# Score products of the last query block as halves of the TensorE array

## The chip, the cores and the metric

The kernel runs on one core of a Trainium2 chip. A core has five engines that work side by side and meet through semaphores: TensorE (PE, matmuls, with its weight loads shown apart as PEld), VectorE (DVE), ScalarE (ACT), GpSimd (POOL) and SyncE (SP). Each takes its instructions in order. SP computes nothing; here it issues nearly all transfers between memories. The metric is the device time of one execution in microseconds (us). The median of three runs of the kernel before is 1521.35 us (1520.33 to 1521.79).

## The reference

One layer: multi-head latent attention with 16 heads over 2048 tokens of width 512, a residual and a layer norm, then one linear map with a residual and a layer norm. The part that matters here:

```python
cq = rms_norm(hidden_states @ w_qa.T, q_a_ln_w)
q = (cq @ w_qb.T).reshape(b, s, H, DQ).transpose(0, 2, 1, 3)
q_nope, q_pe = (q[..., :DN], q[..., DN:])          # 128 and 64 wide
q_pe = q_pe * cos + rotate_half(q_pe) * sin
ckv = hidden_states @ w_kva.T
k_pe = ... the same rotation of ckv[..., KVLR:], one for all heads
scores = jnp.einsum('bhqd,bhkd->bhqk', q_full, k_full) * scale
scores = jnp.where(causal, -jnp.inf, scores)
attn = jax.nn.softmax(scores.astype(jnp.float32), axis=-1)
out = jnp.einsum('bhqk,bhkd->bhqd', attn, v)
```

## The kernel before

**Number format.** Everything that enters a matmul is a float32 value split into a high and a low float16 part; a product is the sum of high by high, high by low and low by high. The key's up-projection is folded into the query, so all heads share one key table `Kn` (128 rows, high and low) and one rotary table `Kp` (64 rows, written twice: rows 0 to 63 and 64 to 127 hold the same values, high in plane 0 and low in plane 1). A head's rotary query `pe` has its high part in rows 0 to 63 and its low part in rows 64 to 127.

**Blocks.** Queries are worked on in four blocks `b` of 512 (`units`, from L981). Block `b` sees `512 (b + 1)` keys. Within a block the loop runs over 8 pairs `p` of heads, then over four query tiles `qt` of 128, then over the two heads `j` of the pair. One pass of the inner loop is called a head below: 64 of them in block 3, 8 in a pair. In block 3 a head has 1664, 1792, 1920 or 2048 keys for `qt` 0 to 3.

**One head** (`head_scores`, L712). `chunks` cuts the keys into two tiles of two chunks: 512 and 512 columns, then twice 320, 384, 448 or 512. A tile is two PSUM banks. In block 3 three such tiles take turns (`"ssu"[state["turn"]]`), so the second tile of a head is the first tile of the head before it. For each chunk `score` (L680) issues five matmuls of 128 rows: `Kn` high and low with the high query, `Kn` high with the low query, `Kp` high and low with the rotary query. The causal mask is a sixth small matmul for `j = 0` (L695) and an addition on DVE for `j = 1` (L699). DVE then takes each tile's row maximum (L738), a small step makes the bias (L748), ACT takes the exponentials (L754) and sums, DVE the reciprocal (L766, L767).

**The head before it** (`head_probs`, L770) is finished in between: ACT writes the high half of the probabilities (L775, two halves of the row), DVE the low half (L778, two halves), and SP issues one DMA transpose of both into a ring (L782), from which TensorE later takes the products with the values (`values`, L820, matmuls in L831). After the transpose `put_in` issues stores that were put off.

**The order of the work.** In block 3, from `(b, p, qt) = (3, 0, 1)` on, the instructions of TensorE, SP, DVE and ACT stand in the order in which the Python code issues them. For head n this is: its scores on TensorE; on DVE the first maximum, with `qt > 1` the first low half of head n - 1, the second maximum, the bias, the remaining low halves of n - 1; the transpose of n - 1 on SP; the exponentials of n on ACT. Then come `run_soon` (rotary low parts on ACT and POOL), `fill` (a piece of the projections of the next pair: `project_pe` L607, `project_nope` L657) and one half of a `values` product. A projection's rotary rows are gathered by POOL into `pe`.

Of the kernel before, what the change touches and what calls it, by code (L numbers as in the profile page):

```python
# [9 lines left out]
F16 = mybir.dt.float16  # L10
BF16 = mybir.dt.bfloat16
F32 = mybir.dt.float32
F32R = mybir.dt.float32r
AF = mybir.ActivationFunctionType
ALU = mybir.AluOpType
# [4 lines left out]
P = 128  # L20
# [6 lines left out]
QB = 512  # L27
NPAIR = H // 2
# [8 lines left out]
W_O = 32768.0  # L37
X_UP = 1024.0
PROBS = 10240
TINY = 1.0e-30  # L40
NEG = -1.0e30

# [16 lines left out]
def mla_block(ctx: ExitStack, tc: tile.TileContext, a, out):  # L59
    nc = tc.nc  # L60
# [33 lines left out]
    identb = const.tile([P, P], BF16, name="identb")  # L94
    nc.vector.tensor_copy(identb, ident)
    maskb = const.tile([P, P], BF16, name="maskb")
# [28 lines left out]
    Kn = kv.tile([P, 2, S], F16, name="Kn")  # L125
    Kp = kv.tile([P, 2, S], F16, name="Kp")
# [14 lines left out]
    psum = {}  # L141
# [366 lines left out]
    state = {"queue": nc.sync}  # L508
# [85 lines left out]
    def run_soon():  # L594
        while soon:
            soon.pop(0)()
# [104 lines left out]

    def take(n):

        at = state.get("probs_at", 0)
        if at + n > PROBS:
            at = 0
        state["probs_at"] = at + n
        return probs_mem[:, at : at + n]  # L710

    def head_scores(pools, b, p, j, qt, nk, prev):  # L712
        r = er[1][:, p // 2 : p // 2 + 1]
        cks = chunks(nk)
        nt = len(cks)
        neg = small.tile([P, 2], F32, tag="neg", name="neg")
        tiles = []
        for ti, ck in enumerate(cks):

            if b == 2 and ti == 1:  # L720
                ps = psum["t"].tile([P, 1, 512], F32, tag="t", name=f"s{b}_{p}_{qt}_{j}_{ti}", bufs=2)
            else:
                k = "s"
                if b == 3:

                    state["turn"] = (state.get("turn", -1) + 1) % 3
                    k = "ssu"[state["turn"]]
                ps = psum[k].tile(
                    [P, 2, 512], F32, tag=k, name=f"s{b}_{p}_{qt}_{j}_{ti}", bufs=3 if b == 1 else 1 if k == "u" else 2
                )  # L730
            w = ck[0][1]
            for ci, (c0, w) in enumerate(ck):
                d = nk - P - c0
                score(ps[:, ci, :], c0, w, b, p, j, qt, d if 0 <= d < w else None)
            v = ps[:, : len(ck), :w]
            if ti == nt - 1 == 0:
                next(prev, None)
            nc.vector.tensor_reduce(neg[:, ti : ti + 1], v, axis=AX.XY, op=ALU.max, negate=True)  # L738
            tiles.append((v, ck[0][0], len(ck), w))
            if ti < nt - 1:  # L740
                next(prev, None)
                if b < NB - 1 or qt > 1 and (p, qt, j) != (NPAIR - 1, 3, 1):
                    next(prev, None)
        bias = small.tile([P, 1], F32, tag="bias", name="bias")
        if nt == 1:
            nc.vector.tensor_scalar(bias, neg[:, 0:1], r, None, ALU.mult)
        else:
            nc.vector.tensor_scalar(bias, neg[:, 0:1], neg[:, 1:2], r, ALU.min, ALU.mult)  # L748
        for _ in prev:
            pass  # L750
        pr = take(nk)
        sums = small.tile([P, 2], F32, tag="sums", name="sums")
        for ti, (v, c0, n, w) in enumerate(tiles):
            nc.scalar.activation(  # L754
                pr[:, c0 : c0 + n * w].rearrange("p (a c) -> p a c", a=n),
                v,
                AF.Exp,
                bias=bias,
                scale=r,
                accum_out=sums[:, ti : ti + 1],  # L760
            )
        inv = small.tile([P, 1], F32, tag="inv", name="inv")
        if nt == 1:
            nc.vector.tensor_scalar(inv, sums[:, 0:1], 1.0 / P_UP, None, ALU.mult)
        else:
            nc.vector.tensor_scalar(inv, sums[:, 0:1], sums[:, 1:2], 1.0 / P_UP, ALU.add, ALU.mult)  # L766
        nc.vector.reciprocal(inv, inv)  # L767
        return pr, inv
# [114 lines left out]
    with tc.manual_schedule(engines={ET.PE}):  # L883
# [38 lines left out]
        pe = state["pe", 0, 0] = blk.tile([P, 4, QB], F16, tag="pe", name="pe0_0")  # L922
# [58 lines left out]
    def units(pool, ring, b, norms=None):  # L981
        lag = min(ring.shape[1] // (2048 * (b + 1)) - 1, 3) if b else 4

        for p in range(NPAIR):
            put_in(True)


            if p + 1 == NPAIR:
                at = (1, 2, 4, 5) if b < NB - 1 else (1, 3, 5, 7)
            elif p % 2 == 0 and p + 2 < NPAIR:  # L990
                at = (0, 1, 2, 3) if (b, p) == (1, 0) else (0, 1, 3, 4)
            else:
                at = (3, 4)
            if b and p % 2 == 0 and p + 2 < NPAIR:
                fillers.append(project_pe(b, p // 2 + 1))
            if p + 1 < NPAIR:
                fillers.append(project(b, p + 1) if b == 0 else project_nope(b, p + 1))
            elif b + 1 < NB:
                fillers.append(project(b + 1, 0))
            if b == NB - 1 and p == NPAIR - 1:  # L1000
                ctx_p.close()
                pcr = state["pcr"] = ctx.enter_context(
                    tc.tile_pool(name="pcr", bufs=2, side="right", reuse_waits="tile")
                )
                state["wvo"] = [pcr.tile([P, 2, 2, HID], F16, name=f"wvo{p}", bufs=1) for p in range(EARLY)]
                for i in range(EARLY):
                    fillers.append(value_output(i, psum["m"], "m"))
                at = (2, 3, 5, 6)
            for qt in range(4):
                nk = (4 * b + qt + 1) * P  # L1010
                if (b, p, qt) == (NB - 1, 0, 1):
                    ctx_f.enter_context(tc.manual_schedule(engines={ET.PE, ET.SP, ET.DVE, ET.Activation}))
                if (b, p) == (0, NPAIR - 1) and qt >= 2:
                    spare = state["qn", 0, p][:, 2:] if qt == 2 else state["pe", 0, 3][:, 4:]
                    s0 = -4 * nk
                    PT = spare.rearrange("p a b c -> p (a b c)" if qt == 2 else "p a b -> p (a b)")[:, : 4 * nk]
                elif b == 0:
                    s0, PT = -4 * nk, pool.tile([P, 4 * nk], F16, tag=f"PT{qt}", name=f"PT{p}_{qt}")
                else:
                    s0 = room(2048 * (b + 1), ring.shape[1], 4 * nk, (b, p) == (2, NPAIR - 1) and qt > 0)  # L1020
                    PT = ring[:, s0 : s0 + 4 * nk]
                vg = values(b, p, qt, nk, PT)
                if nk <= 512:
                    pi = pair_scores(pool, b, p, qt, nk)
                    probs.append(pair_probs(pool, b, p, qt, nk, PT, *pi))
                    flush()
                    for step in plan[p][qt]:
                        if step == "F":
                            fill()
                        else:  # L1030
                            next(side[step == "W"], None)
                    move_rows(6)
                    run_values(lag)
                    run_values(lag)
                else:
                    for j in range(2):
                        prepare_output(b, p, 2 * qt + j)
                        prev = probs.pop() if probs else iter(())
                        pi = head_scores(pool, b, p, j, qt, nk, prev)
                        probs.append(head_probs(pool, b, p, j, qt, nk, PT, *pi))  # L1040
                        if (b, p, qt, j) == (1, 0, 1, 0):
                            half_values()
                            half_values()
                        run_soon()
                        if 2 * qt + j in at:
                            fill()
                        if b == 2 and (2 * qt + j) % 4 == 2:
                            next(norms, None)
                        run_values(lag)
                vals.append([vg, 0, s0, s0 + 4 * nk])  # L1050
                if b == 0 and qt == 3 and p + 2 < NPAIR:
                    if p % 2 == 0:
                        load_wpe(0, p // 2 + 1)
                    load_wq(0, p + 2)
            drain()
        if b:
            flush()
# [92 lines left out]
    while len(vals) > 2:  # L1150
# [5 lines left out]
    ring = ctx_m.enter_context(tc.tile_pool(name="rings", bufs=1, reuse_waits="tile")).tile(  # L1156
        [P, 12 * 2048], F16, name="ring"
    )
    probs_mem = ctx_m.enter_context(tc.tile_pool(name="probs", bufs=1, reuse_waits="tile")).tile(
        [P, PROBS], F32, name="probs"  # L1160
    )
# [239 lines left out]
```

## Time and profile before

| what | value |
|---|---|
| median of three runs | 1521.35 us |
| the profiled execution, its own time | 1521.0 us |
| its span, first to last instruction | 1519.2 us |
| granted TensorE clock, mean | 0.990 |
| block 3, first score matmul to the end of the last one | 817.1 to 1269.8 us |
| TensorE busy in block 3 | 446.60 of 452.70 us |
| instructions in the trace | 24663 |

The profile is of one execution. Its page gives the busy time of each engine, the chain of work that ended last, followed back from the last instruction, and the costliest groups of instructions by source line. Other views give one engine's instructions in order of time (start, duration, engine, line, operation, what is written and read, and in brackets the idle time before and what ended it), or the busy time of every engine in a stretch, with the granted clock (PEclk) and the share of the DMA engines. A matmul's duration contains its way through the array; the distance between two starts says how fast the array takes them. DMA instructions appear on SP's queue (SPq) with the time for which they occupy it; a transfer lands later.

### The profile page before, as it was taken

The numbers are of one execution on the slowest core, as the hardware profiler recorded it, in microseconds if no ns is written. First come the engines' busy times: TensorE is split into PE (matmuls) and PEld (weight loads), VectorE is DVE, ScalarE is ACT, GpSimd is POOL, SyncE is SP. The second block draws the span as 40 slices with busy tenths as digits, with TensorE's granted clock in tenths as the row PEclk, the third lists the DMA queues.
The fourth block names the chain that finished last, engine by engine and source line by source line (L and its number), as shares of the span: only waits on it lengthen the run. The fifth ranks groups of instructions, "written<-read, shape, count | busy, mean of one in ns | idle before, by whom it ended". The sixth has DMA issues, their size and how long they took to land.

```text
span 1519.2 us, 24663 instructions
## 1 busy us (share of the span) xinstructions
PE 1463.0 (96%) x9116; PEld 915.3 (60%) x9116; DVE 1168.2 (77%) x2181; ACT 938.5 (62%) x1695; POOL 347.3 (23%) x404
## 2 busy tenths in 40 slices
PE   8889988999999999999999999999999989999997
PEld 6667754666665566666666666666666655444445
DVE  5797788888887888888887877877878766465664
ACT  6687775666676777777775675676667665322310
POOL 4223211452216305050033401401300000032132
PEclk9899999999999999999999999999999999999999
DMA  5568774879797898989897788787788798634410
GB/s 202 152 168 202 177 184 108 161 154 173 154 195 152 154 198 177 186 183 180 150 203 146 149 154 164 149 154 153 144 152 183 137 212 186 225 125 127 136 49 35
DMA packets 626536, 242.96 MB, mean 160 GB/s; under 512 B 583024, under 2 KB 603760, under 8 KB 625776
## 3 DMA queue, kind: packets, MB, share of 16 engines
q1 hardware_dynamic: 624960, 239.52, 72.8%
q8 instruction: 71, 1.16, 0.3%
q10 hardware_dynamic: 1152, 1.31, 0.3%
q0 software_dynamic: 304, 0.56, 0.1%
q14 instruction: 49, 0.40, 0.1%
HBM read 67.57 MB, written 28.05 MB: 63 GB/s over the span
## 4 chain that ended last, share of the span: by engine, by line
PE 61%; DVE 3%; DMA 2%; ACT 1%; issue 1%; SPq 0%; POOL 0%; POOLq 0%; ACTq 0%; DVEq 0%
PE s L693 26%; PE o L831 17%; PE acc L1134 10%; PE ps_qn L651 4%; PE ff L1279 3%; PE ps_pe L564 2%; DVE probs L778 1%; DVE neg L738 1%; PE ps_wo L297 1%; ACT probs L754 1%; DMA ring<-probs 1%; DMA fraw<-in_fw_dram 1%; PE tp L1270 0%; DMA wo<-in_wo_dram 0%; ACT probs L775 0%
## 5 line engine op out<-in xcount | busy, mean ns | idle before, releaser
L693 PE MATMUL s<-Kn,qn 128*128 128x512 f16 (+5 forms) x1920 | 462.9, 347 | 10.2 <-DVE qn L73 4.4
L754 ACT ACTIVATE probs<-s,bias,er 128x1024 f32<-128x1024 f32 (+3 forms) x320 | 324.4, 1017 | 209.4 <-DVE bias L748 73.0
L778 DVE SCALAR_TENSOR_TENSOR probs<-probs,inv 128x1024 f16<-128x1024 f32 (+7 forms) x320 | 355.3, 1131 | 26.1 <-ACT probs L775 23.2
L831 PEld LDWEIGHTS <-V 128*128 128x128 f16 x3264 | 319.8, 98 | 86.3 <-issue 12.9
L831 PE MATMUL o<-ring,V 128*128 128x256 f16 x3024 | 362.6, 273 | 2.3 <-DMA ring<-probs 2.0
L738 DVE TENSOR_REDUCE neg<-s 128x1 f32<-128x1024 f32 (+3 forms) x320 | 317.2, 993 | 46.3 <-PE s L693 42.8
L693 PE MATMUL s<-Kp,pe 128*128 128x512 f16 (+5 forms) x1280 | 340.1, 347 | 0.0
L775 ACT ACTIVATE probs<-probs,inv 128x1024 f16<-128x1024 f32 (+7 forms) x320 | 294.2, 959 | 71.1 <-DVE inv L767 52.3
L693 PEld LDWEIGHTS <-qn 128*128 128x128 f16 x1920 | 187.5, 98 | 154.7 <-issue 13.9
L693 PEld LDWEIGHTS <-pe 128*128 128x128 f16 x1280 | 124.8, 98 | 105.8
L651 PE MATMUL ps_qn<-cq,wq 128*128 128x512 f16 (+1 forms) x594 | 138.9, 382 | 5.7 <-DVE qn L73 2.9
L638 POOL TENSOR_TENSOR pe<-prod,ph 32x512 f16<-32x512 f32 x88 | 123.8, 1406 | 5.7
L1134 PE MATMUL acc<-wvo,oh 128*128 128x512 f16 (+1 forms) x424 | 124.1, 375 | 0.9 <-ACT probs L754 0.9
L629 POOL TENSOR_TENSOR prod<-prod 128x512 f32<-128x512 f32 x11 | 14.0, 1269 | 457.4 <-DVE prod L569 457.4
L651 PEld LDWEIGHTS <-wq 128*128 128x128 f16 x594 | 59.3, 100 | 68.1 <-issue 9.3
L1134 PE MATMUL acc<-wvo,ol 128*128 128x512 f16 (+1 forms) x212 | 79.5, 375 | 0.0
L766 DVE TENSOR_SCALAR inv<-sums 128x1 f32<-128x1 f32 x128 | 26.9, 210 | 65.8 <-ACT probs L754 65.2
L564 PE MATMUL ps_pe<-cq,wpe 128*128 128x512 f16 (+1 forms) x306 | 69.5, 373 | 7.4 <-ACT ot L836 4.4
L836 ACT ACTIVATE ot<-o 128x256 f32<-128x256 f32 x128 | 48.4, 379 | 40.7 <-PE o L831 30.1
L72 ACT ACTIVATE xt<-tp 128x512 f16<-128x512 f32 (+1 forms) x17 | 9.7, 572 | 100.3 <-PE tp L1270 86.4
L1134 PEld LDWEIGHTS <-oh 128*128 128x128 f16 x424 | 41.5, 98 | 49.0 <-issue 5.2
L633 POOL CAST pe<-prod 32x512 f16<-32x512 f32 x88 | 66.4, 755 | 12.1 <-PE o L831 8.7
(210 smaller groups left out, 1583.0 us busy)
## 6 DMA issues: line engine op xcount, KB each, us to landing
ot_d<-ot SPq DMA_DIRECT2D x128, 128.0 KB, 2.6
o<-ot_d SPq DMA_DIRECT2D x32, 512.0 KB, 3.7
wq<-wq_d SPq DMA_DIRECT2D x30, 384.0 KB, 3.7
wpe<-wpe_d SPq DMA_DIRECT2D x15, 384.0 KB, 3.9
nw<-in_wo_dram SPq DMA_DIRECT2D x8, 512.0 KB, 4.2
wo<-in_wo_dram SPq DMA_DIRECT2D x4, 1024.0 KB, 6.2
x<-in_x_dram SPq DMA_DIRECT2D x16, 256.0 KB, 3.5
out_dram<-xb SPq DMA_DIRECT2D x15, 256.0 KB, 2.0
```

The lines of the kernel that those rows point to most:

```text
L564: nc.tensor.matmul(ps, w[:, i, lt, x * P : (x + 1) * P], cq[:, tiles(cols), k, lt], start=n == 0, stop=n == 3 * LT - 1)
L633: nc.gpsimd.tensor_copy(pe[32 * x : 32 * x + 32, j, :], rp[q, x, :])
L638: nc.gpsimd.tensor_tensor(pe[64 + 32 * x : 96 + 32 * x, j, :], rp[q, x, :], ph[q, 0, x, :], ALU.subtract)
L651: nc.tensor.matmul(ps, w[:, i, lt, j * P : (j + 1) * P], cq[:, tiles(cols), k, lt], start=n == 0, stop=n == 3 * LT - 1)
L693: nc.tensor.matmul(ps[:, :w], lhs, K[:, i, c0 : c0 + w], start=n == 0, stop=n == 4)
L738: nc.vector.tensor_reduce(neg[:, ti : ti + 1], v, axis=AX.XY, op=ALU.max, negate=True)
L754: nc.scalar.activation(pr[:, c0 : c0 + n * w].rearrange("p (a c) -> p a c", a=n), v, AF.Exp, bias=bias, scale=r, accum_out=sums[:, ti : ti ...
L775: nc.scalar.activation(hl[:, 0, c], pr[:, c], AF.Copy, scale=inv)
L778: nc.vector.scalar_tensor_tensor(hl[:, 1, c], pr[:, c], inv, hl[:, 0, c], ALU.mult, ALU.subtract)
L831: nc.tensor.matmul(ps[:, :256], vt[:, k % 4, i, :], v[:, :, l, k, :], start=n == 0, stop=n == 3 * kts - 1)
L836: nc.scalar.activation(ot, ps[:, :256], AF.Copy)
L1134: nc.tensor.matmul(acc[:, cols], l[:, t, c], state["wvo"][p][:, i, j, cols], start=p == 0 and j == 0 and n == 0, stop=p == NPAIR - 1 and j ...
```

## The change

In block 3 (`b >= ROWS`, with `ROWS = 3`) `head_scores` takes both tiles of a head first and hands all four chunks to a new function. It issues half matmuls of 64 rows: two chunks at a time, one on the lower half of the array's rows, one on the upper half. Each chunk needs nine: both halves of the three `Kn` terms and of the `Kp` high term, and one of the `Kp` low term (the rotary high part only). A chunk's halves must reach its PSUM bank from both sides of the array, so there are two passes: chunks (0, 1), then (2, 3), each with five halves a chunk; then (1, 0) and (3, 2), with four. Between a chunk's two passes an instruction without work on SP reads the bank in name: it waits for the first pass, and the second pass waits for it. In the compiled program these are semaphore instructions on SP; both of head n + 1 stand behind the DMA transpose of head n - 1.

For the upper rows the rotary high part is also needed in rows 64 to 127. `rope_again` copies it there by a DMA on SP once a pair (64 rows of 1024 elements), issued in the second head of the pair before. The mask's matmul comes after all score products, its addition on DVE before the first maximum instead of before the second. The rest of the order of DVE and ACT, and all of POOL, is as before. TensorE has 1024 more matmuls and as many more weight loads.

```diff
+ROWS = 3
+    def rope_again(b, p):
+        again = state["again", b, p] = psum["again"].tile([P, 2, QB], F16, tag="again", name=f"again{b}_{p}")
+        nc.sync.dma_start(again[64:], state["pe", b, p // 2][:64, 2 * (p % 2) : 2 * (p % 2) + 2])
+
+    def scores_by_rows(parts, b, p, j, qt, masked):
+        qs = slice(qt * P, (qt + 1) * P)
+        qn = state["qn", b, p]
+        high, low = qn[:, 0, j, qs], qn[:, 1, j, qs]
+        rope, again = state["pe", b, p // 2][:, 2 * (p % 2) + j, qs], state["again", b, p][:, j, qs]
+        upper = [slice(0, 64), slice(64, P)]
+        left = {n: 9 for n in range(4)}
+        left[3] += masked is not None
+        last = set()
+
+        def add(n, lhs, rhs):
+            ps, c0, w = parts[n]
+            begin = n not in last
+            left[n] -= 1
+            return nc.tensor.matmul(ps[:, :w], lhs, rhs, start=begin, stop=left[n] == 0)
+
+        for lanes in ((0, 1), (2, 3), (1, 0), (3, 2)):
+            first = lanes[0] < lanes[1]
+            ops = [(high, Kn, 0), (high, Kn, 1), (low, Kn, 0), (rope, Kp, 0)]
+            if first:
+                ops.append((None, Kp, 1))
+            for at, (lhs, K, i) in enumerate(ops):
+                for lane, n in enumerate(lanes):
+                    c0, w = parts[n][1:]
+                    rows = upper[lane]
+                    w_ = lhs if lhs is not None else (rope, again)[lane]
+                    ins = add(n, w_[rows], K[rows, i, c0 : c0 + w])
+                    last.add(n)
+            if first:
+                nc.sync.keepalive_nop([nc.sync.lower_ap(parts[n][0][:, : parts[n][2]]) for n in lanes])
+        if masked is not None:
+            ps = parts[3][0]
+            nc.tensor.matmul(ps[:, masked : masked + P], identb, maskb, start=False, stop=True)
...
+        if b >= ROWS:
+            made, parts = [], []
+            for ti, ck in enumerate(cks):
+                state["turn"] = (state.get("turn", -1) + 1) % 3
+                k = "ssu"[state["turn"]]
+                ps = psum[k].tile([P, 2, 512], F32, tag=k, name=f"s{b}_{p}_{qt}_{j}_{ti}", bufs=1 if k == "u" else 2)
+                made.append(ps)
+                parts += [(ps[:, ci], c0, w) for ci, (c0, w) in enumerate(ck)]
+            d = nk - P - parts[3][1]
+            scores_by_rows(parts, b, p, j, qt, d if j == 0 else None)
+            if j:
+                dg = parts[3][0][:, d : d + P]
+                nc.vector.tensor_tensor(dg, dg, maskb, ALU.add)
         for ti, ck in enumerate(cks):
-            if b == 2 and ti == 1:
+            if b >= ROWS:
+                ps = made[ti]
+            elif b == 2 and ti == 1:
...
+                        if b >= ROWS and (qt, j) == (0, 1) and p + 1 < NPAIR:
+                            rope_again(b, p + 1)
+                        if b == ROWS - 1 and p == NPAIR - 1 and (qt, j) == (3, 0):
+                            rope_again(ROWS, 0)
...
+    psum["again"] = ctx_m.enter_context(tc.tile_pool(name="again", bufs=2, reuse_waits="tile"))
```

More of the change, by code (lines that the diff above doesn't have):

```diff
@@ L39 @@
 PROBS = 10240
+ROWS = 3
+SYNC = mybir.DependencyInfo(mybir.DependencyClass.Sync, mybir.DependencyReason.DATA)
 TINY = 1.0e-30
@@ L732, in head_scores @@
             for ci, (c0, w) in enumerate(ck):
+                if b >= ROWS:
+                    continue
                 d = nk - P - c0
```

## The prediction

> **What bounds the kernel now.** I read the page's header and chain first, then block 3 alone by windows, then SP's queue and one DVE stretch in order of time, and last the windows around the few places where TensorE stood still.
>
> ```profile
> PE 1463.0 (96%) x9116; PEld 915.3 (60%) x9116; DVE 1168.2 (77%) x2181; ACT 938.5 (62%) x1695; POOL 347.3 (23%) x404
> PE 61%; DVE 3%; DMA 2%; ACT 1%; issue 1%; SPq 0%; POOL 0%; POOLq 0%; ACTq 0%; DVEq 0%
> ```
>
> TensorE is busy nearly throughout, and the chain that ends last is its own work. SP has no share in it. In block 3 (first row; then pairs 1 and 2 alone) this is sharper:
>
> ```profile
> 817.10:1269.80 452.70, 446.60 (x2867) 280.46 (x2865) 354.06 (x508) 298.82 (x439) 60.86 (x54) 0.99 0.80 158
> 873.40:928.00 54.60, 54.60 (x359) 34.68 (x357) 42.55 (x63) 36.98 (x54) 0.00 (x0) 1.00 0.84 157
> 928.00:986.50 58.50, 58.50 (x377) 36.45 (x375) 47.15 (x67) 37.92 (x55) 20.27 (x18) 1.00 0.79 153
> ```
>
> The stretch is its first figure, TensorE's busy time the second: a pair of heads takes 56.55 us on the mean of an odd and an even one, all of it TensorE. So any time saved on TensorE counts, and any new wait of TensorE counts too. The change brings such a wait, on SP, so SP's queue matters:
>
> ```profile
> L782 SPq DMA_TRANSPOSE ring<-probs x64: 3614/4492/7202, 819.3 to 1267.2; - x64
> ```
> ```profile
> 951.91 3.90 SPq L782 DMA_TRANSPOSE ring<-probs  x1
> 955.86 0.57 SPq L522 DMA_DIRECT2D ot_d<-ot  x1
> ...
> 1149.95 4.49 SPq L782 DMA_TRANSPOSE ring<-probs  x1
> 1154.49 0.57 SPq L522 DMA_DIRECT2D ot_d<-ot  x1
> 1157.40 4.68 SPq L782 DMA_TRANSPOSE ring<-probs  x1
> 1162.18 0.60 SPq L522 DMA_DIRECT2D ot_d<-ot  x1
> ```
>
> The line before this second fence gives the least, median and greatest time of block 3's 64 transposes; the rows are start, duration, instruction. A transpose holds SP 4.49 us, and what is next starts 0.05 us after its end: SP is in order and busy while a transpose is issued. Today no compute engine waits on SP itself, only on transfers that have landed.
>
> **The change, part by part.** *Fewer slots.* A head's scores are 20 matmuls, five per key chunk. Rows of 512 columns start 216 ns apart (five from 879.41 to 880.49 us), of 320 columns 136 ns; for 384 and 448 columns I take 163 and 189. Afterwards they are 36 half matmuls in 18 pairs. Per pair of heads the scores take 2 x 5 x (4 x 2 x 0.216 + 2 x (0.136 + 0.163 + 0.189 + 0.216)) = 31.4 us; a tenth is 3.1 us, over 8 pairs 25 us, if a pair takes one slot. No row shows two halves at once. The ends are 216 ns (wholly together) and 432 ns (one after the other); I take 216, the only slot the rows have, and keep 432 for the range. The 16 additional weight loads a head (98 ns each) run beside matmuls, as 60% of the span already does; a 128-column matmul with its load takes some 55 ns (the mask's, 989.72 to 989.77 us), so two loads and two matmuls fit in a slot of 136 ns. Switching between whole and half array is bounded by nothing and by one matmul's drain, 379 - 216 = 163 ns, twice a head; it falls into the idle time found below.
>
> [...]
>
> *The new wait.* The first pass puts chunk 0 on the lower and chunk 1 on the upper rows (5 pairs), then chunks 2 and 3 (5 pairs); the second pass swaps lanes (4 + 4). Before each swap TensorE waits for an SP no-operation, which waits for the first pass. In SP's order both no-operations of head n+1 stand behind the transpose of head n-1, because that transpose is put in after the scores of head n. It waits for the second low-part split (L778) of n-1 on DVE, which stands behind both maxima (L738) of head n, and the maximum of the first tile needs its second pass. So a ring closes: second pass of n, maxima of n, splits of n-1, transpose of n-1 on SP, no-operation of n+1, second pass of n+1. Before, no step of TensorE hung on SP.
>
> DVE's steps in their present order:
>
> ```profile
> 1153.09 1.28 DVE L778 SCALAR_TENSOR_TENSOR probs<-probs,inv 128x1024 f16<-128x1024 f32 x1 [0.16 <-ACT probs L775]
> 1154.29 0.29 DVE L699 TENSOR_TENSOR s<-s,maskb 128x128 f32<-128x128 f32 x1
> 1154.62 1.22 DVE L738 TENSOR_REDUCE neg<-s 128x1 f32<-128x1024 f32 x1
> 1155.88 0.27 DVE L748 TENSOR_SCALAR bias<-neg,er 128x1 f32<-128x1 f32 x1
> 1156.07 1.27 DVE L778 SCALAR_TENSOR_TENSOR probs<-probs,inv 128x1024 f16<-128x1024 f32 x1
> ```
>
> *The ring's time for a pair of heads (8 heads).* Second pass on tile one, 8 x 4 x 0.216 = 6.9. For the four heads with j = 1 the mask is now added before the first maximum, so both tiles must be finished: 4 x (0.216 + 0.189 + 0.163 + 0.136) = 2.8, and the addition 4 x 0.33 = 1.3. From TensorE's last slot to DVE, 0.16 of drain and 0.04 of handover: 1.6. Maxima 8 x 1.22 + 2 x (0.82 + 0.96 + 1.09 + 1.22) = 18.0. Bias 8 x 0.27 = 2.2. Two splits a head, by the group rows of these two pairs (1146, 1359, 1211, 1278 ns for 832, 896, 960, 1024 elements), 4 each: 20.0. Transposes 8 x 4.49 = 35.9. Behind them four stores of 0.62, a wq load of 0.43, half a wpe load and the new copy of the rotary high rows (one per pair, 128 KB, taken like a store): 3.8. Handovers, some 0.35 a head by the gaps of 0.03 to 0.05 between these rows: 2.8. The sum is 95.3 us against 56.55: 38.75 more, over 8 pairs 310 us.
>
> Nothing covers this: TensorE's own work is 56.55 - 3.1 = 53.4 us a pair, so it would idle 42 us, some 5 us a head. The 25 us saved on it lie in that idle time, and so do values and projections. DVE, ACT and DMA do the same work with more room. The copies' data is ready (POOL fills a rotary group in the even pair before, and is at 0.00 in pair 1, where the first such copy stands), and the first one, in block 2, delays SP by about 0.6 us that nobody waits for.
>
> *The clock.* Idle TensorE loses its clock (third figure from the right: PEclk):
>
> ```profile
> 242.10:245.50 3.40, 0.00 (x0) 0.00 (x0) 3.05 (x8) 0.08 (x1) 0.00 (x0) 1.00 0.84 193
> 245.60:248.90 3.30, 3.04 (x8) 1.12 (x8) 0.67 (x3) 2.81 (x7) 0.00 (x0) 0.50 0.12 40
> ```
>
> After a gap of 4.40 us the next 3.4 us ran at half clock, eight matmuls in 3.40 us. Pauses of 5 us a head would repeat that. In the ring only the second passes can slow down: between 0 and 6.9 + 2.8 = 9.7 us a pair, 0 to 78 us in all. I take half, 39 us, since the half-clock stretch need not meet the second pass.
>
> [...]
>
> The profiled execution took 1521.0 us (span 1519.2), the median of the runs is 1521.35. 1521.0 + 310 + 39 = 1870.
>
> **The rivals.** *A, halves do not overlap.* 432 ns a pair: second passes grow by 9.7 us a pair, 78 us, to 103.6 a pair, still above TensorE's own 53.4 + 28.3; 1948, more with half clock. Nothing in this trace speaks for or against it.
>
> *B, transposes hold SP for less once they come alone.* For: their times vary (3614 to 7202). Against: 951.91 came 4.9 us after the one before and still took 3.90, no less than its size mostly takes. At three quarters 72 us less, about 1800; at half, about 1725.
>
> *C, the SP wait costs nothing, and PSUM alone binds.* A head's second tile is the first tile of the head before, free after its exponential. It is now wanted 5 slots after the scores begin (1.08 us), not 10, and the maxima come later. For a j = 1 head of 2048 keys: 13 pairs 2.8, drain 0.26, mask 0.33, maximum, split, maximum 3.7, bias 0.39, exponential with its handover 1.35 make 8.8 us against 6.6 now; with j = 0, 7.6 against 6.7. With the like for shorter rows and the larger of ring and TensorE for each head, about 60.3 us a pair: +30 us, 1551. It needs SP free when the no-operation is due, which the 4.49 us speak against.
>
> *D, faster.* All new waits lie beside other work and the 25 us come: 1496. The place is the no-operation: it decides for this if SP reaches it within the 5 pairs of the second group, 1.08 us, and C's ring is also covered.
>
> **How the numbers follow.** My forecast 0.58, its own range 1800 to 1930; A 0.18; B 0.13; C 0.07; D 0.03; no visible change 0.01. A tenth more or less on the transposes moves the sum by 29 us. Below 1760 lie C, D, no change and a little of B (0.13), above 1960 part of A (0.06). A measurement of this kernel tells 0.2%, 3 us, from no change: faster 0.03, same 0.01, slower 0.96.
>
> **What would show it.** Right: in block 3 a pair of heads near 95 to 100 us; TensorE busy about 60% there and idle in front of swapped passes, released by SP; no-operations on SP starting right after a transpose ends; PEclk clearly under 0.99 in block 3; transposes still near 4.5 us; blocks 0 to 2 unchanged to within 3 us. Halves overlapping show as pairs starting a few ns apart and slots of 216 ns. Wrong: pairs of heads near 60 us (C) or 53 us (D), or slots of 432 ns (A), or transposes clearly under 4 us (B).

## The result, and the profile after

The changed kernel takes 1836.93 us (median of four runs, 1832.17 to 1839.1); the kernel before took 1521.36 us beside it. The ratio is 1.207, with a 95% interval of 1.205 to 1.210: 316 us slower. The profiled execution took 1839.1 us, its span is 1837.3 us and its mean granted clock 0.923 (before 0.990).

The head of the page of the changed kernel: busy time and instructions of each engine, and the chain that ended last by engine.

```profile
PE 1558.5 (85%) x10140; PEld 929.8 (51%) x10140; DVE 1160.4 (63%) x2181; ACT 937.8 (51%) x1695; POOL 335.2 (18%) x404
PE 31%; SPq 11%; DVE 5%; issue 4%; ACT 3%; POOL 0%; POOLq 0%; ACTq 0%; DVEq 0%
```

SP's queue, which had 0% of the chain, now has 11%. TensorE's share of the span fell from 96% to 85%, and yet its busy time rose by 95 us. The reason shows in block 3 by windows (stretch, its length, busy time of PE, PEld, DVE, ACT and POOL, then PEclk, the share of the DMA engines, GB/s). The first row is the whole block, the second goes from the first exponential of pair 1 to that of pair 3, so two pairs of heads:

```profile
814.80:1586.60 771.80, 541.53 (x3902) 294.48 (x3901) 347.92 (x512) 302.13 (x444) 49.49 (x54) 0.83 0.48 96
924.20:1116.70 192.50, 138.98 (x988) 75.34 (x986) 87.34 (x129) 74.87 (x109) 16.49 (x18) 0.84 0.47 93
```

In the kernel before, block 3 begins 2.7 us earlier than the 817.1 us named ahead of the prediction: its first head, the first with chunks of 320 columns, starts at 814.42. That kernel's TensorE in order of time, and the whole block by windows:

```profile
814.42 0.81 PE L693 MATMUL s<-Kn,qn 128*128 128x512 f16 x3
816.58 0.57 PE L693 MATMUL s<-Kn,qn 128*128 128x320 f16 x3
```
```profile
814.40:1269.80 455.40, 449.30 (x2881) 281.85 (x2880) 354.66 (x512) 301.00 (x443) 60.86 (x54) 0.99 0.80 158
```

So block 3 took 455.40 us and now takes 771.80, 316 more; what lies ahead of it is as long as before to 0.4 us, and what lies behind is 1.3 us longer. Two pairs took 113.1 us (54.60 + 58.50) and now take 192.5. DVE and ACT are busy for about as long as before: they do the same work and wait longer. The granted clock is 0.83, so some 260 us of the block, (1 - 0.83) x 2 x 771.8, ran at half clock (PEclk 0.50), where the pairs of half matmuls of 512 columns in the second passes start 0.43 us apart, the second 0.38 us behind the first, instead of 0.215.

The waits of the changed kernel between 820 and 1580 us (who waited for whom: sum in us, times, longest):

```profile
PE s L726 <- SPq L741: 204.5, 61, 8.5
DVE s L772 <- PE s L726: 186.8, 30, 8.7
DVE neg L797 <- PE s L726: 162.4, 33, 6.8
PE s L726 <- ACT probs L813: 19.8, 16, 1.9
```

L726 is the half matmuls, L741 the no-operations, L772 the mask's addition, L797 the maxima. 61 of the 64 heads wait on SP in this stretch, 3.4 us each, and DVE waits for the scores once a head: by the mask's addition (about half of the heads) or by the first maximum. Now one head in order of time, SP's queue first, then TensorE, then DVE (start, duration, instruction, and in brackets the idle time before and what ended it):

```profile
1204.47 4.80 SPq L841 DMA_TRANSPOSE ring<-probs  x1
1209.36 0.54 SPq L524 DMA_DIRECT2D ot_d<-ot  x1
1216.76 4.83 SPq L841 DMA_TRANSPOSE ring<-probs  x1
```
```profile
1202.10 0.59 PE L726 MATMUL s<-Kp,pe 64*128 64x512 f16 x3
1202.32 0.38 PE L726 MATMUL s<-Kp,again 64*128 64x512 f16 x1
1204.64 0.58 PE L726 MATMUL s<-Kn,qn 64*128 64x320 f16 x6 [1.94 <-ACT probs L813]
...
1210.00 1.47 PE L726 MATMUL s<-Kn,qn 64*128 64x512 f16 x6 [4.50 <-SPq L741]
1211.23 0.66 PE L726 MATMUL s<-Kp,pe 64*128 64x512 f16 x2
```
```profile
1200.49 1.28 DVE L837 SCALAR_TENSOR_TENSOR probs<-probs,inv 128x1024 f16<-128x1024 f32 x1
1201.68 1.22 DVE L797 TENSOR_REDUCE neg<-s 128x1 f32<-128x1024 f32 x1
1202.93 0.27 DVE L807 TENSOR_SCALAR bias<-neg,er 128x1 f32<-128x1 f32 x1
1203.12 1.27 DVE L837 SCALAR_TENSOR_TENSOR probs<-probs,inv 128x1024 f16<-128x1024 f32 x1
...
1211.93 1.23 DVE L797 TENSOR_REDUCE neg<-s 128x1 f32<-128x1024 f32 x1 [5.71 <-PE s L726]
```

This is the ring. The second split ends at 1204.39 and the transpose starts at 1204.47. The first pass ended at about 1205.5, but the transpose holds SP until 1209.27 and the store behind it until 1209.90. Only then come the no-operations, and the second pass starts at 1210.00. The first maximum at 1211.93 waits for that pass, and the next split and transpose wait for the maxima. The wait of 1.94 us at 1204.64 is a second, smaller ring: the tile for chunks 2 and 3 is wanted five slots after the scores begin, before the exponential of the head before has freed it.

### The profile page after: what moved, and what is told of

Same layout as the page of the kernel before. It is cut to its first block, busy times and chain, and to the rows that moved or that the text cites. A ratio compares the mean times of both kernels' runs of the same rounds, so it can differ in the third digit from the quotient of the medians.

```text
span 1837.3 us, 26856 instructions
## 1 busy us (share of the span) xinstructions
PE 1558.5 (85%) x10140; PEld 929.8 (51%) x10140; DVE 1160.4 (63%) x2181; ACT 937.8 (51%) x1695; POOL 335.2 (18%) x404
## 3 DMA queue, kind: packets, MB, share of 16 engines
q1 hardware_dynamic: 625600, 240.57, 60.3%
## 4 chain that ended last, share of the span: by engine, by line
PE 31%; SPq 11%; DVE 5%; issue 4%; ACT 3%; POOL 0%; POOLq 0%; ACTq 0%; DVEq 0%
PE s L726 12%; SPq L841 10%; PE acc L1197 9%; PE o L890 5%; ACT probs L813 3%; PE ff L1343 2%; DVE probs L837 2%; DVE neg L797 2%; PE ps_qn L653 1%; SPq L524 1%; PE ps_wo L299 1%; PE ps_pe L566 1%; PE tp L1334 0%; PE s L744 0%; DVE qn L75 0%
## 5 line engine op out<-in xcount | busy, mean ns | idle before, releaser
L726 PE MATMUL s<-Kn,qn 64*128 64x512 f16 (+3 forms) x1536 | 244.8, 430 | 228.2 <-SPq L741 208.3
L797 DVE TENSOR_REDUCE neg<-s 128x1 f32<-128x1024 f32 (+3 forms) x320 | 316.2, 993 | 181.4 <-PE s L726 162.4
L890 PE MATMUL o<-ring,V 128*128 128x256 f16 x3024 | 380.5, 281 | 1.5 <-DMA ring<-probs 1.2
L890 PEld LDWEIGHTS <-V 128*128 128x128 f16 x3264 | 327.0, 101 | 97.8 <-issue 24.0
L695 PE MATMUL s<-Kn,qn 128*128 128x512 f16 (+5 forms) x1152 | 268.9, 340 | 9.7 <-DVE qn L75 4.4
L726 PEld LDWEIGHTS <-qn 64*128 64x128 f16 x1536 | 85.8, 106 | 338.8 <-issue 295.8
L695 PE MATMUL s<-Kp,pe 128*128 128x512 f16 (+5 forms) x768 | 198.0, 340 | 0.0
L695 PEld LDWEIGHTS <-qn 128*128 128x128 f16 x1152 | 112.4, 98 | 86.4 <-issue 11.5
L726 PE MATMUL s<-Kp,pe 64*128 64x512 f16 (+3 forms) x640 | 139.0, 416 | 0.0
L772 DVE TENSOR_TENSOR s<-s,maskb 128x128 f32<-128x128 f32 x32 | 9.6, 299 | 192.5 <-PE s L726 192.5
L695 PEld LDWEIGHTS <-pe 128*128 128x128 f16 x768 | 74.7, 98 | 58.1
```

The source lines that it names most:

```text
L695: nc.tensor.matmul(ps[:, :w], lhs, K[:, i, c0 : c0 + w], start=n == 0, stop=n == 4)
L726: return nc.tensor.matmul(ps[:, :w], lhs, rhs, start=begin, stop=left[n] == 0)
L890: nc.tensor.matmul(ps[:, :256], vt[:, k % 4, i, :], v[:, :, l, k, :], start=n == 0, stop=n == 3 * kts - 1)
```

## The experiments

Theory T: the time goes to the wait on SP, behind a transpose that hangs on the second pass before it; halves as such cost little. Rival H: halves of 64 rows cost the time themselves. "Before" ran on the same chip in each case: 1521.1 to 1521.5 us. Where no number of runs stands, there was one; runs of one kernel lay up to 7 us apart here.

**Whole-array matmuls with the same wait.** Every product is 128 rows again, in two passes of three and two products; the no-operations stay.

```diff
-            ops = [(high, Kn, 0), (high, Kn, 1), (low, Kn, 0), (rope, Kp, 0)]
-            if first:
-                ops.append((None, Kp, 1))
+            ops = [(high, Kn, 0), (high, Kn, 1), (low, Kn, 0)] if first else [(rope, Kp, 0), (rope, Kp, 1)]
...
-                    ins = add(n, w_[rows], K[rows, i, c0 : c0 + w])
+                    add(n, lhs, K[:, i, c0 : c0 + w])
```

> No halves at all: block 3 multiplies with all 128 rows (20 slots a head), but in the same two passes (three products a chunk, then two) and with the same two no-operations on SP. Theory (the wait on SP behind the transposes is the cost): the ring is the one of the changed kernel, its second pass on the first tile again four slots of 216 ns, so block 3 stays near 770 us and the time near 1837 us (1815 to 1860). Rival H (the half matmuls themselves cost the time, by their weight loads or the switching of the array): without them the time falls to 1521 to 1570 us.

Measured: 1819.57 us. Its windows row for block 3 and its wait (815 to 1566 us):

```profile
814.20:1566.40 752.20, 530.28 (x2877) 304.93 (x2876) 347.47 (x510) 301.60 (x442) 50.46 (x54) 0.88 0.48 98
```
```profile
PE s L726 <- SPq L739: 198.5, 62, 10.0
```

Without a single half matmul nearly all of the loss is there. H falls.

**The same without the wait.** With whole matmuls both passes add to a bank in order, so the no-operation can go.

```diff
-                nc.sync.keepalive_nop([nc.sync.lower_ap(parts[n][0][:, : parts[n][2]]) for n in lanes])
+                pass
```

> As e1 and without the no-operations: full matmuls in two passes, no wait. It prices rival C alone, the later maxima and the earlier claim on the PSUM tile. Theory: heads of 1920 and 2048 keys go to the ring over the exponential, 7.9 and 8.6 to 9.0 us instead of 6.3 to 6.7; the sum for a pair of heads is 62.7 us against 56.55, so 1570 us (1550 to 1585). Rival: if the order of the passes costs nothing, 1521 us; if it costs as much as the changed kernel lost, 1837 us.

Measured: 1556.68 us. Between these two kernels only the wait differs: 262.9 us. What stays above the kernel before, 35.5 us, belongs to what is left of the change, the order of the passes above all, and the mask's earlier place. Its wait on the second tile (815 to 1305 us) is of that size, and one case of it stands in order of time below: six products of chunks 0 and 1, then a stop until the tile is free.

```profile
PE s L726 <- ACT probs L811: 33.9, 24, 1.9
```
```profile
985.24 1.46 PE L726 MATMUL s<-Kn,qn 128*128 128x512 f16 x6
988.44 1.46 PE L726 MATMUL s<-Kn,qn 128*128 128x512 f16 x6 [1.74 <-ACT probs L811]
```

**The changed kernel, with its no-operations on POOL** instead of SP:

```diff
-                nc.sync.keepalive_nop([nc.sync.lower_ap(parts[n][0][:, : parts[n][2]]) for n in lanes])
+                nc.gpsimd.keepalive_nop([nc.gpsimd.lower_ap(parts[n][0][:, : parts[n][2]]) for n in lanes])
```

> The changed kernel with its two no-operations on POOL instead of SP. Theory: the ring over the transposes is open, rival C's ring is left: 60.3 us a pair of heads, 1551 us, and up to 60 us more where no-operations queue behind POOL's rotary work (20 us in three of the pairs): 1545 to 1610 us. Rival H (halves are dear wherever the wait is): it stays near 1837 us.

Measured: 1573.85 us. The halves, both passes and the wait for the first pass are all still there; only the queue in which the no-operation stands is another. That alone takes 263 us off the change. Its waits (815 to 1322 us), and two windows, an even pair of heads and the odd one after it:

```profile
PE s L726 <- ACT probs L813: 33.5, 23, 1.9
PE s L726 <- POOLq L741: 15.3, 6, 4.6
```
```profile
950.90:1020.90 70.00, 59.87 (x512) 35.44 (x511) 45.08 (x67) 37.78 (x55) 17.91 (x18) 0.95 0.65 130
1020.90:1079.10 58.20, 53.72 (x478) 31.65 (x477) 42.19 (x63) 36.88 (x55) 0.00 (x0) 1.00 0.78 150
```

The even pair, in which POOL has rotary work (17.91 us), takes 70.0 us, the odd one 58.2; in the kernel before an even and an odd pair took 58.50 and 54.60, by the rows in the prediction. So the no-operation can wait in POOL's queue too, where that queue has work; it has work in every second pair only. TensorE's own work has hardly become less: two pairs (892.8 to 1020.9) hold 113.50 us of it, against 113.10 before, and at the granted clock of 0.97 there the half clock makes at most 3.8 us of it. So at least 109.7 us are left, 1.7 us a pair saved at the most, where the prediction had 3.1. The last two experiments show a cost that takes half of the 3.1.

**The transpose put behind the no-operations**, which stay on SP: the transpose of head n - 1 is issued after the scores of head n + 1.

```diff
+        while held:
+            held.pop(0)()
...
+        def turn():
             nc.sync.dma_start_transpose(
...
+        if b >= ROWS and (p, qt) < (NPAIR - 1, 2):
+            held.append(turn)
+        else:
+            turn()
```

> The changed kernel with the transpose of head n-1 put on SP after the no-operations of head n+1 instead of before them; everything else as it is. Theory: the no-operation then stands behind an older transpose, which starts when the first pass of the head before ends and has about 5.8 us (second pass, values, first pass) for its 4.5 and a store's 0.6; the ring opens and rival C's 60.3 us a pair are left: 1551 us (1540 to 1590). Rival (not the order on SP): 1837 us.

Measured: 1582.64 us, above the 1551 named and inside the range. The wait on SP (815 to 1331 us) fell from 204.5 to 22.4 us:

```profile
PE s L726 <- ACT probs L815: 33.5, 23, 1.9
PE s L726 <- SPq L741: 22.4, 12, 8.2
```

Queue and place both break the ring. The same transposes run here without that cost; what costs is that the no-operation stands behind them. Why 32 us more are left than named is not shown; the wait that remains on SP is of that order.

**More work for TensorE.** Four half pairs of the first pass of chunks 2 and 3 are issued twice more ahead of the real ones, and what they compute is overwritten.

```diff
-        for lanes in ((0, 1), (2, 3), (1, 0), (3, 2)):
+        for turn, lanes in enumerate(((0, 1), (2, 3), (2, 3), (2, 3), (1, 0), (3, 2))):
...
+            idle = turn in (1, 2)
+            if idle:
+                for lhs, K, i in ((high, Kn, 0), (high, Kn, 1), (low, Kn, 0), (rope, Kp, 0)):
+                    for lane, n in enumerate(lanes):
+                        ps, c0, w = parts[n]
+                        nc.tensor.matmul(ps[:, :w], lhs[upper[lane]], K[upper[lane], i, c0 : c0 + w], start=True, stop=True)
+                continue
```

> The changed kernel with additional work for TensorE: four pairs of half matmuls on chunks 2 and 3 are issued twice more before they count, and overwritten (8 slots, 1.1 to 1.7 us a head, 90 us over block 3), in the place where TensorE waits 3.3 us a head for SP. Theory: TensorE's work is free there, and the shorter pause keeps its clock more often; of the 49 us that the second passes lose to the half clock (6.2 us a pair of heads in the changed kernel's trace) half or more come back: 1790 to 1815 us, with PEclk in block 3 above 0.83. Rival 1 (the clock costs nothing, TensorE's work is free): 1837 us. Rival 2 (TensorE's work counts): 1927 us.

Measured: 1815.26 us, 21.7 us less than the changed kernel with 1024 more matmuls. Block 3 and the wait (815 to 1566 us):

```profile
815.10:1562.90 747.80, 581.20 (x4928) 333.63 (x4927) 349.57 (x512) 302.24 (x444) 51.83 (x54) 0.94 0.50 99
```
```profile
PE s L726 <- SPq L748: 135.8, 60, 6.5
```

The clock in block 3 rose from 0.83 to 0.94. That the second passes, which lie on the ring, run faster shows when the ring is cut at the start of each second pass and at the first maximum behind it (heads 8 to 55, us per pair of heads):

| kernel | clock in block 3 | second pass to first maximum | from there to the next second pass |
|---|---|---|---|
| changed | 0.83 | 18.7 | 78.2 |
| whole matmuls, same wait | 0.88 | 16.4 | 77.8 |
| changed, more work | 0.94 | 14.2 | 78.7 |

The three differ by up to 4.5 us a pair in the second pass, and by at most 0.9 us in all the rest. So at least some 22 of the 316 us are the clock's, and the 17 us by which the first experiment, with two slots more of work a head, was faster than the changed kernel lie in the same place.

**The mask late.** The kernel with its no-operations on POOL, and the mask's addition back in front of the second maximum, so that the first needs only its own tile.

```diff
-            if j:
-                dg = parts[3][0][:, d : d + P]
-                nc.vector.tensor_tensor(dg, dg, maskb, ALU.add)
...
+            if b >= ROWS and j and ti == nt - 1:
+                dg = parts[3][0][:, d : d + P]
+                nc.vector.tensor_tensor(dg, dg, maskb, ALU.add)
...
             nc.vector.tensor_reduce(neg[:, ti : ti + 1], v, axis=AX.XY, op=ALU.max, negate=True)
```

> e3 (no-operations on POOL, 1573.9 us) with the mask's addition put back before the second maximum, so that the first maximum of a j = 1 head need not wait for chunks 2 and 3. Theory (part of rival C's price is this order): the ring over the exponential gets shorter by the second pass on the second tile and the addition, 0.9 to 1.2 us, in the j = 1 heads of 1920 and 2048 keys, and by 0.6 in those of 1664: 3.0 us a pair, 24 us, so 1550 us (1543 to 1558). Rival (POOL's queue is what e3 has left, not the order of the maxima): 1574 us.

Measured: 1565.2 us, 8.7 us less: between the two expectations. The mask's place is worth a third of what was thought. The wait for the second tile fell by as much (24.2 us here, 33.5 with the mask early), and what is left of it is over half of the 44 us that this kernel still lies above the one before.

**One pass.** What can halves bring without any of the waits? Four whole products a chunk, and only the last term (rotary high by `Kp` low, which needs 64 rows) as one half pair a tile. Nothing has to reach a bank from both sides in a second pass, so there is no no-operation, and the tiles are taken as before.

```diff
+        for n, (ps, c0, w) in enumerate(parts):
+            for at, (lhs, K, i) in enumerate(((high, Kn, 0), (high, Kn, 1), (low, Kn, 0), (rope, Kp, 0))):
+                nc.tensor.matmul(ps[:, :w], lhs, K[:, i, c0 : c0 + w], start=at == 0, stop=False)
...
+        for n, (ps, c0, w) in enumerate(parts):
+            rows, w_ = ((slice(0, 64), rope), (slice(64, P), again))[n]
+            nc.tensor.matmul(ps[:, :w], w_[rows], Kp[rows, 1, c0 : c0 + w], start=False, stop=True)
```

> The saving without the swap: per chunk four full matmuls as before, and only the product with the low rotary keys as half matmuls, chunk 0 or 2 on the lower rows beside chunk 1 or 3 on the upper ones. 18 slots a head, tiles one after the other, the mask as before, no no-operation, the copy of the rotary rows as in the changed kernel. Theory: nothing closes a ring over SP; TensorE saves 25 us of slots, but in heads of 1920 and 2048 keys the chain over maxima and exponentials (6.9 to 7.35 us a head in the trace before, against 6.3 to 6.7 of TensorE) takes part of it back: 1496 to 1513 us, faster than before. Rival H (each switch between full and half array drains it, 163 ns, four times a head, 42 us): 1530 to 1540 us, slower than before.

Measured: 1524.07 us (11 runs), ratio 1.0022 (1.0013 to 1.0031): no gain, a little slower, and between the two expectations. TensorE in order of time:

```profile
984.95 0.81 PE L719 MATMUL s<-Kn,qn 128*128 128x512 f16 x3
985.60 0.38 PE L719 MATMUL s<-Kp,pe 128*128 128x512 f16 x1
985.91 0.39 PE L724 MATMUL s<-Kp,pe 64*128 64x512 f16 x1
985.91 0.39 PE L724 MATMUL s<-Kp,again 64*128 64x512 f16 x1
986.23 0.82 PE L719 MATMUL s<-Kn,qn 128*128 128x512 f16 x3
```

Three whole products take 985.60 - 984.95 = 0.65 us, 0.216 each. From the whole to the half pair it is 0.31 us, and from the half pair to the next whole 0.32 us, both about 0.10 us more. A head goes over four times, 0.40 us, and that is the 0.27 to 0.43 us which its two slots save: TensorE is busy for 450.06 us of block 3 (816.4 to 1273.2), and was for 449.30. Block 3 grew by 1.4 us here; where the rest of the 3 us lies is not shown.

**One change of form instead of two**, that is, to halves and back once a head. Order within a head: whole products of tile one, half pair of tile one, half pair of tile two, whole products of tile two. `halves()` issues the half pair of a tile; the edit is shown against the kernel of the last experiment.

```diff
+        if ti == 1:
+            halves()
         for n, (ps, c0, w) in enumerate(parts):
...
-        for n, (ps, c0, w) in enumerate(parts):
-            rows, w_ = ((slice(0, 64), rope), (slice(64, P), again))[n]
-            nc.tensor.matmul(ps[:, :w], w_[rows], Kp[rows, 1, c0 : c0 + w], start=False, stop=True)
+        if ti == 0:
+            halves()
```

> As the run with four whole products and one half pair a tile, but a head goes over from the whole array to halves and back once instead of twice: whole products of tile one, half pair of tile one, half pair of tile two, whole products of tile two. Theory (each change of the array's form costs about 0.10 us of TensorE, as 0.312 and 0.319 us instead of 0.216 us between starts showed there): a head saves two slots (0.27 to 0.43 us, mean 0.35) and pays 0.20 us, so 0.07 to 0.23 us a head, mean 0.15, times 64 heads = 10 us: 1511 us (1505 to 1516). Rival 1 (the change of form is not what ate the gain there; the chain maximum - exponential - tile binds): as that run, 1522 to 1526. Rival 2 (a change costs more when two half pairs stand between): above 1526.

Measured: 1517.62 us (7 runs) against 1521.53, ratio 0.9973 (0.9962 to 0.9984). This one beats the kernel before by 3.9 us, where 10 were expected; 1517.62 lies just outside the range. Its TensorE in order of time, the waits of TensorE for scores' tiles (814 to 1267 us), and block 3 by windows:

```profile
993.38 0.38 PE L727 MATMUL s<-Kp,pe 128*128 128x512 f16 x1
993.70 0.39 PE L721 MATMUL s<-Kp,pe 64*128 64x512 f16 x1
993.70 0.39 PE L721 MATMUL s<-Kp,again 64*128 64x512 f16 x1
993.92 0.30 PE L721 MATMUL s<-Kp,pe 64*128 64x320 f16 x1
993.92 0.30 PE L721 MATMUL s<-Kp,again 64*128 64x320 f16 x1
994.15 0.58 PE L727 MATMUL s<-Kn,qn 128*128 128x320 f16 x3
```
```profile
PE s L721 <- ACT probs L794: 5.3, 8, 0.9
PE s L721 <- DMA again<-pe: 1.2, 1, 1.2
```
```profile
814.60:1266.30 451.70, 439.15 (x2882) 260.28 (x2880) 356.33 (x512) 300.88 (x443) 59.80 (x54) 0.99 0.83 162
```

Between the two half pairs the distance is the plain slot, 0.22 us, so each change of form costs its 0.10 us once. TensorE's busy time in block 3 fell from 449.30 to 439.15 us, the 10 us expected, but block 3 only from 455.40 to 451.70. Of the 10 us, 4.8 went into the wait for the second tile (5.3 us; 0.5 in the kernel before), which is now wanted a slot earlier and in a head that is shorter, and 1.2 into the first copy of the rotary rows. That leaves 4.

Half matmuls in two passes with no wait at all between the passes were not tried: both halves of the array would add to one bank with nothing to order them.

## Why the prediction was right

The forecast was 1870, the measurement 1836.93 us: the likeliest case, inside its own range, with a sum 33 us too high. By its steps:

**The ring, and that nothing covers it: right.** All four links show in order of time above. The pair with and without the no-operation (1819.57 and 1556.68 us), and the no-operation in another queue or place (1573.85 and 1582.64), put 254 to 263 us on the wait in SP's queue.

**A slot of 216 ns for a pair of halves: right.** In the changed kernel the two pairs of rotary halves above (three `pe` and one `again`) start at 1202.10 and 1202.32; in the last two experiments both halves of a pair start at the same time to 10 ns. Two halves together therefore take the time of one whole product (0.22 us here, 0.216 for a whole one). Rival A falls; its 103.6 us a pair was mis-added (95.3 + 9.7 = 105.0), and nothing rested on it.

**The ring's sum: 4.5 us a pair of heads too long.** Over heads 8 to 55 I cut each head by starts of instructions. Per pair of heads, beside the prediction's terms:

| stage | predicted | measured |
|---|---|---|
| second pass and what ends it, at full clock | 12.6 | 12.5 |
| half clock in it | 4.9 (39 / 8) | 6.2 |
| maxima, bias, splits, transposes, what SP does behind them, handovers | 82.7 | 78.2 |
| sum | 100.2 | 96.9 |

The transposes are as predicted, 8 x 4.49 = 35.9 against 35.4, though each now comes alone (median 4444 ns; rival B falls):

```profile
L841 SPq DMA_TRANSPOSE ring<-probs x64: 3611/4444/5330, 819.6 to 1578.4; - x64
```

What failed is the term for DVE, where I added up durations and then handovers: recorded durations of neighbours overlap. The split at 1200.49 lasts 1.28 us, to 1201.77, but the maximum behind it starts at 1201.68. From start to start it is mostly 0.08 us less than the duration, not 0.03 to 0.05 more. The rows in the prediction had it already: the bias at 1155.88 lasts 0.27 us, to 1156.15, and the split behind it starts at 1156.07. From the first maximum to the transpose the handovers came to -0.9 us a pair, where 2.8 stood for the whole ring. The splits were also a little shorter (1084 to 1276 ns a group, 19.0 instead of 20.0 us a pair); what lies behind a transpose, with its handovers, took 4.6 us instead of 3.8. 4.5 us over 8 pairs are 36 us too many. With the 10 us too few for the clock below, that is 26 of the 33; the rest lies outside heads 8 to 55.

**The clock: right in kind, 10 us too low.** 6.2 us a pair make 49 us in place of 39, which was an estimate, half of 78. In 32 of the 48 heads the second pass on tile one ran at half clock. When the clock fell can be read from the traces. In those of the kernel before and of the changed kernel all changes of the granted clock, 13 and 105, lie on a grid of 3.413 us, to 1 ns; its edges stand differently against the program's start in the two (the first at 3.21 and at 0.50 us). Cut along this grid, these are windows of the changed kernel: around the pause shown above, then around one of 2.75 us ahead of 1342.00 that was followed by slots of 0.41 us (mean of three), then around one of 3.74 us ahead of 907.00 that was followed by slots of 0.215 us:

```profile
1201.99:1205.40 3.41, 1.47 (x18) 0.73 (x13) 2.37 (x3) 2.11 (x3) 0.00 (x0) 1.00 0.00 0
1205.40:1208.81 3.41, 0.09 (x2) 0.00 (x0) 0.38 (x2) 2.83 (x5) 0.00 (x0) 0.50 1.03 197
1208.82:1212.23 3.41, 2.23 (x14) 1.05 (x15) 0.30 (x1) 0.00 (x0) 0.00 (x0) 0.50 0.69 148
```
```profile
1338.53:1341.94 3.41, 0.72 (x10) 0.29 (x6) 0.00 (x0) 1.70 (x2) 0.00 (x0) 1.00 1.12 213
1341.94:1345.35 3.41, 3.35 (x17) 1.32 (x17) 0.14 (x1) 0.00 (x0) 0.00 (x0) 0.50 0.33 80
```
```profile
901.62:905.03 3.41, 1.64 (x14) 0.64 (x11) 0.46 (x3) 2.87 (x6) 0.00 (x0) 1.00 0.68 130
905.03:908.45 3.42, 1.45 (x14) 0.79 (x15) 0.00 (x0) 0.84 (x1) 0.00 (x0) 1.00 0.95 197
```

In block 3 of these two traces the clock of a window went with TensorE's busy time in the window before it. It fell 47 times, always behind a window with 0 to 1.57 us busy, and no window with less than 1.44 us kept it. From half clock it came back only behind windows with 2.63 us or more. So in the head shown the clock fell at 1205.40, just ahead of the pause of 4.50 us, behind the window with 1.47 us busy; it stayed down behind the next one, which holds most of the pause and 0.09 us busy. The pause of 3.74 us ahead of 907.00 is split by an edge of the grid, both windows had 1.44 us or more busy (1.64 and 1.45), and the clock stayed. So windows that were idle only in part were followed by half clock too, not the wholly idle one in the prediction's rows alone. The kernel before has one such case in block 3:

```profile
1225.20:1228.60 3.40, 0.82 (x6) 0.30 (x4) 0.00 (x0) 1.16 (x2) 0.00 (x0) 1.00 1.00 341
1228.60:1232.00 3.40, 1.39 (x2) 0.65 (x3) 3.35 (x4) 1.74 (x2) 0.00 (x0) 0.50 1.15 259
```

**TensorE busy about 60% of block 3: wrong,** it is 541.53 of 771.80, 70%. The step that failed is the idle time of 42 us a pair (measured 28.8): TensorE's work was counted at full clock, 53.4 us a pair or 427 us, but 195 of its 541.53 busy us lay in windows at half clock, and that slowed the work beside the ring (first passes, values, projections) as well as the ring itself. Half of the 195 are 97 of the 114 us too few; most of the other 17 can be the changes of form, by an estimate of twice a head at 0.10 us.

**The saved slots worth nothing: right.** The kernel with whole products and the same wait was even faster, by the clock of its second passes.

**Rival C** is what is left without the wait on SP. It was priced at 60.3 us a pair and 1551 us. Whole products without the wait came to 1556.68, where two pairs took 122.7 us (886.2 to 1008.9), 61.4 each; an odd pair with the wait on POOL came to 58.2, against 54.60 before. Its mechanism, the second tile wanted early, is the largest wait there, its price about right. **Rival D** was priced at 1496 and never in sight: even the best order found reached 1517.62. Of its two slots a head the change of form, a cost that I had put into idle time, took more than half, and the wait for the second tile half of the rest. In the experiment with four changes a head, with TensorE busy for 450.06 of 456.8 us, they took 0.40 us a head and the two slots saved 0.27 to 0.43 us.

## What to carry to other kernels

An instruction without work costs what its queue costs: ask what stands ahead of it in that queue, how long that holds the queue, and whether that work itself hangs on what the instruction releases. Where it does, a ring closes (254 to 263 of the 316 us here), and its length is the sum of its links from start to start, not of the durations. Before splitting matmuls over halves of the array, price each change between whole and half (0.10 us here) against the slots saved, and keep the products of one form together.

## What the runs showed of the hardware

- Going from whole-array to half-array matmuls, or back, took 0.10 us more than a plain step (0.31 and 0.32 instead of 0.216 us between starts at 512 columns, in the experiment with one pass). Half pair to half pair cost nothing extra (0.22 us, in the one with one change of form).
- Adding 1024 matmuls whose results are thrown away made the changed kernel 21.7 us faster (1815.26 instead of 1836.93 us), at a clock of 0.94 instead of 0.83 in block 3.
- In the traces of the kernel before and of the changed kernel all 118 changes of the granted clock lay on a grid of 3.413 us. In block 3 of these, half clock followed windows with TensorE busy for up to 1.57 us of 3.41, full clock none with less than 1.44; from half clock it came back behind 2.63 us or more. A pause of 2.75 us (ahead of 1342.00, 0.72 us busy in its window) was followed by half clock, one of 3.74 us (ahead of 907.00) was not.
- The durations of successive DVE instructions overlapped by 0.08 and 0.09 us in the rows compared above.
